# When side transfers and weight splits run in a linear attention and mixture-of-experts kernel: zeros and w2's copies in k's later quarters, w1 between wk and wv

## The chip, the cores and the metric

The kernel runs on one core of a Trainium2 chip. Its engines are TensorE (PE; PEld is its weight load), VectorE (DVE), ScalarE (ACT), GpSimd (POOL) and SyncE (SP, which only issues transfers). Each works through its own instruction queue in order. The metric is the device time of one execution, in microseconds; less is better.

## The reference

There are 2048 rows (tokens) of 512 values. A linear attention with 32 heads of 64 is followed by a mixture of 8 experts, of which each token uses 2. Everything is float32.

```python
x = hidden_states                                   # 2048 x 512
xn = layernorm(x)
q, k, v = relu(xn @ Wq), relu(xn @ Wk), xn @ Wv      # 2048 x 2048 each
kv = einsum('bhsd,bhse->bhde', k, v)
key_sum = k.sum(axis=2)
normalizer = clip(einsum('bhsd,bhd->bhs', q, key_sum), 1e-6)
x = x + (einsum('bhsd,bhde->bhse', q, kv) / normalizer) @ Wo + bo
xn = layernorm(x)
top_scores, top_idx = top_k(xn @ gate_w.T + gate_b + bias, 2)
gates = softmax(top_scores)
h = silu(einsum('td,ehd->teh', xn, w1) + b1)         # 8 experts, 352 hidden
x = x + sum over the two experts of gate * (h @ w2 + b2)
```

## The kernel before

Products keep float32's precision by splitting each operand into a high and a low half. The high half is a cast on ScalarE, the low half a subtraction on VectorE or GpSimd (`split`, both on L164), and each product is three matmuls (`mm3`, L158 to L160). There are 16 row tiles of 128 rows (`NT`), and k, v and q are worked on in four quarters of 512 columns (`NQ`).

The first part runs `a_step(s)` for s = 0 to 63; j = s // 16 is the quarter and t = s % 16 the row tile. In the first quarter a step also loads x two tiles ahead, normalises the next row tile (`a_norm`, which calls `norm`), transposes it into `xT` and writes its halves to memory (`xnd`); in later quarters the halves are read back a step ahead (`a_xn`, tile `xn_hl`). Each step then does:

- `a_k(s)`: twelve matmuls into `pk`; ScalarE's relu gives k's high half (L283), VectorE the low half (L284) and the running sum `kacc`.
- `a_g(s-1)`: twelve matmuls of the step before, k against xn, into the four banks `g`.
- At t = 2 of the next quarter, `a_kv(j-1)`: wv's slot against `g`, copied out as `kvs`, split and written to memory (`kvd`), and then the sums of k: `kacc` is split into `ka`, two matmuls with `ones` add over the rows into `pks`, and ScalarE copies the result to `ksb`.

Beside these the steps carry work for later. wk's next quarter is loaded at t = 8 and split at t = 9 to 12; wv is loaded at t = 12 and split at t = 13 and 14; in the first quarter GpSimd takes the low halves. The 22 chunks of w1 (512 columns each) are split in the consecutive steps 16 to 37: load a chunk to a `raw` buffer, split it into the one tile `stage`, write both halves to `w1d`. A chunk's load is held until the relu of the step before:

```python
hold([raw_load(("w1", w + 1), w1[:, ts(w + 1, 512)])], k_done[s - 1])
```

`hold` adds an order and no data; `k_done[s]` is the relu of step s.

After step 1 GpSimd gets its preparation, through `Late`, which holds each of its instructions until step 1's relu. In program order the zeros stand in it: 31 transfers of zeros into `out` behind the result rows, 15 into spare blocks of `xs_d` (with one column rewritten for each, in the same tile `zero`), and three copies of w2's experts with their b2 to `w2d`. Their transfers go through the software queue (q0), SP's through the hardware queue (q1).

This first part and the next, where q is worked on for 48 steps, are ordered on each engine by a planner that simulates the program; the program's order is the priority. The last sixteen steps of q and all the experts are ordered by hand. In q's part, `b_x1` loads x and GpSimd adds bo to it (L351); `b_n` uses `ksb`. `a_kv(3)` is called there at s = 1. The spare blocks, the zeros in `out` and `w2d` are read only by the experts.

Of the kernel before, what the change touches and what calls it, by code (L numbers as in the profile page):

```python
# [10 lines left out]
FP = mybir.dt.float32  # L11
# [4 lines left out]
AF = mybir.ActivationFunctionType  # L16
ALU = mybir.AluOpType
# [4 lines left out]
P = 128  # L22
# [4 lines left out]
def linear_attention__then__moe_kernel(  # L27
# [38 lines left out]
    nc = tc.nc  # L66
    S, C = x.shape
# [85 lines left out]
    def aux_bank(name):  # L153
        return ps.tile([P, 512], FP, tag="aux", bufs=2, name=name)
# [11 lines left out]
    def hold(held, behind):  # L166

        after = mybir.DependencyInfo(mybir.DependencyClass.Sync, mybir.DependencyReason.SCHED_ONLY)
        for ins in held:
            tc.add_manual_dep(ins.ins, behind.ins.name, after, reason="order")  # L170

    def words(engine, o, i):

        engine.dma_start(o.bitcast(FP), i.bitcast(FP))
# [30 lines left out]
    def raw_load(key, src):  # L205
        raws[key] = rawp.tile([P, CP], FP, tag="raw", bufs=4, name="raw")[:, 0:512]
        return nc.sync.dma_start(raws[key], src)

    def raw_split(key, hi, lo, on=nc.vector):
        return split(hi, lo, raws.pop(key), on)  # L210
# [4 lines left out]
    load_x(1)  # L215


    def norm(xt, dst):
        sm = const.tile([P, 16], FP, tag="sm", bufs=3, name="sm")
        st, mv, sd, rs = sm[:, 0:6], sm[:, 6:8], sm[:, 8:9], sm[:, 9:10]  # L220
        first = nc.vector.bn_stats(st, xt)
        nc.vector.bn_aggr(mv, st)
        root = nc.scalar.activation(sd, mv[:, 1:2], AF.Sqrt, bias=eps)
        nc.vector.reciprocal(rs, sd)
        last = nc.vector.tensor_scalar(dst, xt, mv[:, 0:1], rs, ALU.subtract, ALU.mult)
        return first, root, last

    def norm_sums(xt, more):
# [25 lines left out]

    def a_norm(t):
        xn = fpb.tile([P, C], FP, tag="xn", bufs=3, name="xn")
        ins = norm(xs.pop(t), xn)
        tp3 = transpose4(xn, "xtp")
        b, tt = divmod(t, TT)
        ins += split(xT[b][:, 0, :, ts(tt, P)], xT[b][:, 1, :, ts(tt, P)], tp3)  # L260
        xns[t] = frw.tile([P, 2, C], FR, tag="xs", bufs=3, name="xn_hl")
        ins += split(xns[t][:, 0, :], xns[t][:, 1, :], xn)
        words(nc.sync, xnd[t], xns[t])
        return ins
# [46 lines left out]
    def a_kv(j):  # L311

        for p0 in range(0, PP, 2):
            pkv = aux_bank("pkv").rearrange("p (a l b) -> p a l b", a=2, l=2)
            for p in range(p0, p0 + 2):
                for c in range(CC):
                    w, g = slot_n[0][:, c], slot_n[1][:, c]
                    nc.tensor.matmul(
                        pkv[:, p - p0], w[:, 0, ts(p, P)], g[:, :, ts(p, P)],
                        start=c == 0, stop=False,  # L320
                    )
                    nc.tensor.matmul(
                        pkv[:, p - p0, 0, :], w[:, 1, ts(p, P)], g[:, 0, ts(p, P)],
                        start=False, stop=c == CC - 1,
                    )
            for r in range(0, P, D):
                o = slice(r, r + D)
                kv = fpb.tile([P, 2, D], FP, tag="kvs", bufs=2, name="kvs")[o]
                nc.scalar.copy(kv, pkv[o, :, 1, o])
                nc.vector.tensor_add(kv, kv, pkv[o, :, 0, o])  # L330
                split(kvt[o, 0, p0 : p0 + 2, o], kvt[o, 1, p0 : p0 + 2, o], kv)
        words(nc.sync, kvd[j], kvt)
        pks = aux_bank("pks")
        ka = frw.tile([P, 2, QW], FR, tag="xs", bufs=3, name="ka")
        split(ka[:, 0, :], ka[:, 1, :], kacc[j])
        for l in range(2):
            nc.tensor.matmul(pks, ones, ka[:, l, :], start=l == 0, stop=l == 1)
        ksb[j] = fpb.tile([P, QW], FP, tag="ksb", bufs=NQ, name="ksb")
        nc.scalar.copy(ksb[j], pks)
# [196 lines left out]
    hold([n0[6]], n0[4])  # L536
    hold([wk0[2][0], wk0[3][0], n0[5]], n0[3])
    n_w1 = W1N // 512
    NC = 2
    k_done = {}  # L540

    def a_step(s):
        j, t = divmod(s, NT)
        if j == 0:
            if t + 2 < NT:
                load_x(t + 2)
            if t + 1 < NT:
                ins = a_norm(t + 1)
                hold([ins[0]], normed[t][2 if t else 4])
                normed[t + 1] = ins  # L550
        if s + 1 >= NT and s + 1 < NQ * NT:
            a_xn(s + 1)

        if t == 8 and j + 1 < NQ:
            for c in range(CC):
                hold([raw_load(("k", j + 1, c), wk[ts(c, P), ts(j + 1, QW)])], k_done[s - 1])
        if t in (9, 10, 11, 12) and j + 1 < NQ:
            c = t - 9
            w = slot_s[(j + 1) % 2]
            raw_split(  # L560
                ("k", j + 1, c), w[:, c, 0, :], w[:, c, 1, :], nc.vector if j else nc.gpsimd
            )
        if t == 9 and j == NQ - 1:
            for c in range(CC):
                raw_load(("q", 0, c), wq[ts(c, P), ts(0, QW)])
        if t in (10, 11, 12, 13) and j == NQ - 1:
            c = t - 10
            raw_split(("q", 0, c), slot_s[0][:, c, 0, :], slot_s[0][:, c, 1, :])
        if t == 12:
            for c in range(CC):  # L570
                raw_load(("v", j, c), wv[ts(c, P), ts(j, QW)])
        if t in (13, 14):
            for c in (2 * t - 26, 2 * t - 25):
                raw_split(
                    ("v", j, c), slot_n[0][:, c, 0, :], slot_n[0][:, c, 1, :],
                    nc.vector if j else nc.gpsimd,
                )

        w = s - NT
        if 0 <= w < n_w1:  # L580
            if w == 0:
                hold([raw_load(("w1", 0), w1[:, ts(0, 512)])], k_done[s - 1])
            raw_split(("w1", w), stage[:, 0, :], stage[:, 1, :])
            for l in range(2):
                words(nc.sync, w1d[l][:, ts(w, 512)], stage[:, l, :])
            if w + 1 < n_w1:
                hold([raw_load(("w1", w + 1), w1[:, ts(w + 1, 512)])], k_done[s - 1])
        k_done[s] = a_k(s)
        if s:
            a_g(s - 1)  # L590
        if j and t == 2:
            a_kv(j - 1)

    for s in range(NC):
        a_step(s)
# [20 lines left out]
    def temp():  # L616
        return fp1.tile([P, CX], FP, tag="f1", bufs=F1B, name="temp")
# [47 lines left out]
    m_all = rc.tile([P, NT, E], BF, name="m_all")  # L665
    nc.vector.memset(m_all, 0.0)
    place = const.tile([P, NT, 2], I32, name="place")

    zero = temp()
    pool.memset(zero[:, 0 : C + 1], 0.0)  # L670
    pool.memset(zero[:, C + 1 : C + 2], -1.0)
    for b in range(NT + NZ):
        pool.dma_start(out[S + b * P : S + (b + 1) * P, :], zero[:, 0:C])
    for b in range(NZ):
        pool.tensor_scalar(zero[:, C + 2 : CX], part, float(2 * S + b * P), None, ALU.add)
        pool.dma_start(xs_b[NB + b], zero)
    for e in range(E2):
        pool.dma_start(w2d[e, 0:HF].bitcast(FP), w2[e])
        pool.dma_start(w2d[e, HF : HF + 1].bitcast(FP), b2[e : e + 1, :])
    gb = temp()[:, 0 : 2 * E].rearrange("p (l e) -> p l e", l=2)  # L680
    pool.dma_start(gb[:, 0, :], gate_b.partition_broadcast(P))
    pool.dma_start(gb[:, 1, :], bias.partition_broadcast(P))
# [18 lines left out]
    pool.tensor_add(b1m, b1h, b1r)  # L701
    pool.memset(area[:, 80 * KB : 84 * KB].bitcast(FP), 0.0)

    for s in range(NC, NQ * NT):
        a_step(s)
    b_x1(0)
    b_x1(1)
    a_g(NQ * NT - 1)
# [154 lines left out]
    for s in range(NS - NT):  # L863
        j, t = divmod(s, NT)
        b_x1(s + 2)
        b_q(s)
        b_n(s)
        if s == 0:
            for p in range(PP):
                load_o(0, p)  # L870
            b_w(0, 0)
        if s == 1:
            a_kv(NQ - 1)
            for p in range(PP):
                if p + 1 < PP:
                    b_w(0, p + 1)
                b_m(0, p)
        if s >= 2:
            b_o(s - 2)
            for _ in b_add(s - 2):  # L880
                pass
        if s >= 1:
            b_t(s - 1)
        if t == 4:
            for c in range(CC):
                raw_load(("q", j + 1, c), wq[ts(c, P), ts(j + 1, QW)])
        if t in (5, 6, 7, 8):
            c = t - 5
            w = slot_s[(j + 1) % 2]
            raw_split(("q", j + 1, c), w[:, c, 0, :], w[:, c, 1, :])  # L890
        if t == 9:
            for p in range(PP):
                load_o(j + 1, p)
        if t in (10, 11, 12, 13):
            b_w(j + 1, t - 10)
            b_m(j + 1, t - 10)
# [346 lines left out]
```

## Time and profile before

| | us |
|---|---|
| median of 3 runs | 1022.81 |
| lowest and highest run | 1021.46, 1025.57 |
| profiled execution: its own time | 1025.18 |
| profiled execution: span from first to last instruction | 1023.4 |
| TensorE busy | 988.2 (97%) |
| VectorE busy | 559.7 (55%) |
| ScalarE busy | 345.1 (34%) |
| GpSimd busy | 190.8 (19%) |
| mean granted TensorE clock | 0.989 |

The durations of single instructions come from the one profiled execution, which ran 2.4 us above the median. A busy TensorE is not TensorE at its peak: matmuls overlap, and a row's duration (0.39 us for 512 columns) is longer than the distance from one start to the next (0.23 us). So steps are measured here from start to start of `pk`'s first matmul. In the timelines, a bracket at a row's end gives the idle time before it and what ended it.

### The profile page before, as it was taken

To read this page: it belongs to the slowest core of one execution; us is meant where nothing else is said; L and a number is where in the kernel's file an instruction comes from. 1 tells how busy PE (TensorE), PEld (TensorE's weight loads), DVE (VectorE), ACT (ScalarE), POOL (GpSimd) and SP (SyncE) were. 2 spreads that over 40 slices of the span, in tenths; PEclk is the share of its full clock that TensorE was granted. 3 is DMA by queue.
4 is the path that set the end of the run, shared out by engine and by line. 5 is a ranking of instruction groups with operands and counts; after the bars stand their busy time and mean duration, and the time that the engine had idled before them with its cause. 6 is when DMAs were issued, how large, how long until landed. Compare 5 with 4: busy or idle time off the path is not lost. (4 is left out here: it accounts for less than half of the span.)

```text
span 1023.4 us, 14704 instructions
## 1 busy us (share of the span) xinstructions
PE 988.2 (97%) x4903; PEld 825.8 (81%) x4903; DVE 559.7 (55%) x1382; ACT 345.1 (34%) x677; POOL 190.8 (19%) x225
## 2 busy tenths in 40 slices
PE   8999999999999999999999999999999989999993
PEld 5878877788888888788888888888888877889983
DVE  7873334453344226758656865766787766223330
ACT  4333222332223114324112411223545546444441
POOL 3653120000000010031000000001333210643354
PEclk9999999999999999999999999999999999999997
DMA  6994877865535242344322332348655697976788
GB/s 224 374 349 168 247 271 248 275 230 192 173 124 160 98 130 97 113 134 154 114 93 93 114 103 91 95 160 277 216 190 208 227 318 229 167 113 109 129 150 130
DMA packets 77898, 181.33 MB, mean 177 GB/s; under 512 B 9576, under 2 KB 12936, under 8 KB 77648
## 3 DMA queue, kind: packets, MB, share of 16 engines
q1 hardware_dynamic: 62240, 131.94, 39.2%
q0 software_dynamic: 15584, 48.44, 18.8%
q8 instruction: 43, 0.70, 0.3%
q14 instruction: 31, 0.25, 0.1%
HBM read 108.98 MB, written 79.83 MB: 184 GB/s over the span
## 5 line engine op out<-in xcount | busy, mean ns | idle before, releaser
L284 DVE SCALAR_TENSOR_TENSOR k<-pk,k 128x512 fp32r<-128x512 f32 x64 | 44.0, 687 | 122.1 <-ACT k L283 121.8
L158 PE MATMUL po<-area,qT 128*128 128x512 f32 x256 | 101.6, 397 | 1.5 <-ACT qT L164 1.5
L158 PE MATMUL pq<-area 128*128 128x512 f32 x256 | 102.6, 401 | 0.0
L158 PE MATMUL pk<-area 128*128 128x512 f32 x256 | 101.2, 395 | 0.8 <-ACT area L164 0.7
L160 PE MATMUL pk<-area 128*128 128x512 f32 x256 | 100.0, 391 | 1.0 <-DVE area L164 1.0
L159 PE MATMUL g<-k,xn_hl 128*128 128x512 f32 x256 | 100.8, 394 | 0.1
L160 PE MATMUL pq<-area 128*128 128x512 f32 x256 | 100.6, 393 | 0.0
L160 PE MATMUL g<-k,xn_hl 128*128 128x512 f32 x256 | 100.4, 392 | 0.0
L159 PE MATMUL pk<-area 128*128 128x512 f32 x256 | 99.9, 390 | 0.5 <-POOL area L164 0.3
L159 PE MATMUL pq<-area 128*128 128x512 f32 x256 | 100.3, 392 | 0.0
L159 PE MATMUL po<-area,qT 128*128 128x512 f32 x256 | 99.8, 390 | 0.0
L160 PE MATMUL po<-area,qT 128*128 128x512 f32 x256 | 98.7, 391 | 0.0
L164 ACT CAST qT<-qtp 128x512 fp32r<-128x512 f32 x64 | 36.7, 587 | 176.1 <-PE qtp L249 176.1
L158 PE MATMUL g<-k,xn_hl 128*128 128x512 f32 x256 | 91.0, 394 | 3.6 <-ACT k L283 3.6
L164 ACT CAST area<-raw 128x512 fp32r<-128x512 f32 x86 | 53.1, 621 | 117.4 <-DMA raw<-in_w 62.9
L164 DVE TENSOR_TENSOR area<-raw,area 128x512 fp32r<-128x512 f32 x77 | 53.6, 703 | 65.5 <-ACT area L164 54.7
L1132 POOL DMA_INDIRECT out<-ys,dest x37 | 58.2, 1573 | 119.6 <-ACT ys L1129 107.9
L351 POOL TENSOR_TENSOR x<-x,bo_b 128x512 f32<-128x512 f32 x16 | 21.4, 1348 | 311.9 <-DMA x<-in_x 306.7
L283 ACT ACTIVATE k<-pk 128x512 fp32r<-128x512 f32 x64 | 38.1, 596 | 121.9 <-PE pk L160 121.7
L369 DVE TENSOR_TENSOR qk<-q,ksb 128x512 f32<-128x512 f32 x64 | 44.4, 694 | 32.3 <-ACT q L361 31.6
L412 DVE TENSOR_TENSOR x<-x,po 128x512 f32<-128x512 f32 x48 | 32.9, 686 | 53.0 <-PE po L160 46.6
L361 ACT ACTIVATE q<-pq 128x512 f32<-128x512 f32 x64 | 38.4, 600 | 66.7 <-PE pq L160 42.5
(225 smaller groups left out, 2092.2 us busy)
## 6 DMA issues: line engine op xcount, KB each, us to landing
xn_hl<-xnd SPq DMA_DIRECT2D x48, 512.0 KB
x1d<-x SPq DMA_DIRECT2D x48, 256.0 KB
x<-x1d SPq DMA_DIRECT2D x48, 256.0 KB
w1d<-area SPq DMA_DIRECT2D x44, 256.0 KB
area<-w1d POOLq DMA_DIRECT2D x16, 704.0 KB
xg<-xs_d SPq DMA_DIRECT2D x37, 257.5 KB
xnd<-xn_hl SPq DMA_DIRECT2D x16, 512.0 KB
out<-temp POOLq DMA_DIRECT2D x31, 256.0 KB
```

The lines of the kernel that those rows point to most:

```text
L158: first = nc.tensor.matmul(o, lh, rh, start=start, stop=False)
L159: nc.tensor.matmul(o, lh, rl, start=False, stop=False)
L160: nc.tensor.matmul(o, ll, rh, start=False, stop=stop)
L164: return nc.scalar.copy(hi, src), on.tensor_sub(lo, src, hi.bitcast(FP))
L283: relu = nc.scalar.activation(k[:, 0, :], pk, AF.Relu)
L284: nc.vector.scalar_tensor_tensor(k[:, 1, :], pk, 0.0, k[:, 0, :].bitcast(FP), ALU.max, ALU.subtract)
L351: nc.gpsimd.tensor_add(x1s[s], x1s[s], bo_b)
L361: nc.scalar.activation(q, pq, AF.Relu)
L369: nc.vector.tensor_mul(qk, q, ksb[j])
L412: nc.vector.tensor_add(x1, x1, pos.pop(s))
L1132: added[i] = nc.gpsimd.indirect_dma_start(out[:, :], bass.IndirectOffsetOnAxis(dest[:, i : i + 1].bitcast(U32), 0), ys, None, compute_op=A ...
```

## The change

It moves work in time and between engines:

- The zeros and w2's copies leave the preparation. They become a list of 49 jobs (3 copies, 15 zero rows, 31 zero results), of which each step from 32 on takes two and holds them until its own relu.
- w1's 22 chunks are split in the steps from 16 on with t in 1, 3 to 8, or 15: 17, 19 to 24, 31, 33, 35 to 40, 47, 49, 51 to 55.
- In the first quarter wk is loaded at t = 5 and split at t = 6 to 9, and wv is loaded at t = 10 and split at t = 11 to 14, one chunk a step. VectorE takes all their low halves.
- The sums of k become `a_ks`, called at t = 6 instead of in `a_kv` at t = 2; for the last quarter at s = 6 of q's part instead of s = 1.
- `norm` gets a flag. For row tiles 6 to 15 the last step (x - mean) * rs is a ScalarE activation with scale rs and bias -mean * rs, and VectorE computes that bias.

```diff
-    def norm(xt, dst):
+    def norm(xt, dst, on_scalar):
...
-        last = nc.vector.tensor_scalar(dst, xt, mv[:, 0:1], rs, ALU.subtract, ALU.mult)
+        if on_scalar:
+            nc.vector.scalar_tensor_tensor(nr, mv[:, 0:1], -1.0, rs, ALU.mult, ALU.mult)
+            last = nc.scalar.activation(dst, xt, AF.Identity, bias=nr, scale=rs)
+        else:
+            last = nc.vector.tensor_scalar(dst, xt, mv[:, 0:1], rs, ALU.subtract, ALU.mult)
...
-        ins = norm(xs.pop(t), xn)
+        ins = norm(xs.pop(t), xn, t > 5)
...
         words(nc.sync, kvd[j], kvt)
+
+    def a_ks(j):
+
         pks = aux_bank("pks")
...
+    w1_steps = [
+        s for s in range(NT, NQ * NT) if s % NT in (1, 3, 4, 5, 6, 7, 8, NT - 1)
+    ][:n_w1]
...
-        if t == 8 and j + 1 < NQ:
+        t_k, t_v = (9, 12) if j else (6, 10)
+        if t == t_k - 1 and j + 1 < NQ:
...
-        if t in (9, 10, 11, 12) and j + 1 < NQ:
-            c = t - 9
+        if t_k <= t < t_k + CC and j + 1 < NQ:
+            c = t - t_k
             w = slot_s[(j + 1) % 2]
-            raw_split(
-                ("k", j + 1, c), w[:, c, 0, :], w[:, c, 1, :], nc.vector if j else nc.gpsimd
-            )
+            raw_split(("k", j + 1, c), w[:, c, 0, :], w[:, c, 1, :])
...
-        if t == 12:
+        if t == t_v:
...
-        if t in (13, 14):
-            for c in (2 * t - 26, 2 * t - 25):
...
+        if t > t_v:
+            parts_v = (t - t_v - 1,) if not j else (2 * (t - t_v) - 2, 2 * (t - t_v) - 1)
...
-        w = s - NT
-        if 0 <= w < n_w1:
-            if w == 0:
-                hold([raw_load(("w1", 0), w1[:, ts(0, 512)])], k_done[s - 1])
+        if s in w1_steps:
+            w = w1_steps.index(s)
             raw_split(("w1", w), stage[:, 0, :], stage[:, 1, :])
...
-            if w + 1 < n_w1:
-                hold([raw_load(("w1", w + 1), w1[:, ts(w + 1, 512)])], k_done[s - 1])
+        if s + 1 in w1_steps:
+            w = w1_steps.index(s + 1)
+            hold([raw_load(("w1", w), w1[:, ts(w, 512)])], k_done[s - 1])
...
+        if j and t == 6:
+            a_ks(j - 1)
...
-    for b in range(NT + NZ):
-        pool.dma_start(out[S + b * P : S + (b + 1) * P, :], zero[:, 0:C])
-    for b in range(NZ):
-        pool.tensor_scalar(zero[:, C + 2 : CX], part, float(2 * S + b * P), None, ALU.add)
-        pool.dma_start(xs_b[NB + b], zero)
-    for e in range(E2):
-        pool.dma_start(w2d[e, 0:HF].bitcast(FP), w2[e])
...
+    later = [
+        *((copy_weights, e) for e in range(E2)), *((zero_rows, b) for b in range(NZ)),
+        *((zero_results, b) for b in range(NT + NZ)),
+    ]
+
     for s in range(NC, NQ * NT):
         a_step(s)
+        if s >= 2 * NT:
+            for job, n in later[:2]:
+                hold(job(n), k_done[s])
+            del later[:2]
...
+        if s == 6:
+            a_ks(NQ - 1)
```

More of the change, by code (lines that the diff above doesn't have):

```diff
@@ L215, in linear_attention__then__moe_kernel @@
     load_x(1)
-    def norm(xt, dst):
+    def norm(xt, dst, on_scalar):
         sm = const.tile([P, 16], FP, tag="sm", bufs=3, name="sm")
-        st, mv, sd, rs = sm[:, 0:6], sm[:, 6:8], sm[:, 8:9], sm[:, 9:10]
+        st, mv, sd, rs, nr = sm[:, 0:6], sm[:, 6:8], sm[:, 8:9], sm[:, 9:10], sm[:, 10:11]
         first = nc.vector.bn_stats(st, xt)
@@ L568, in a_step @@
             raw_split(("q", 0, c), slot_s[0][:, c, 0, :], slot_s[0][:, c, 1, :])
-        if t == 12:
+        if t == t_v:
             for c in range(CC):
                 raw_load(("v", j, c), wv[ts(c, P), ts(j, QW)])
-        if t in (13, 14):
-            for c in (2 * t - 26, 2 * t - 25):
[L574 to L577, printed above, removed]
-        w = s - NT
-        if 0 <= w < n_w1:
-            if w == 0:
-                hold([raw_load(("w1", 0), w1[:, ts(0, 512)])], k_done[s - 1])
+        if t > t_v:
+            parts_v = (t - t_v - 1,) if not j else (2 * (t - t_v) - 2, 2 * (t - t_v) - 1)
+            for c in parts_v:
+                if c < CC:
+                    raw_split(("v", j, c), slot_n[0][:, c, 0, :], slot_n[0][:, c, 1, :])
+        if s in w1_steps:
+            w = w1_steps.index(s)
             raw_split(("w1", w), stage[:, 0, :], stage[:, 1, :])
@@ L667, in linear_attention__then__moe_kernel @@
     place = const.tile([P, NT, 2], I32, name="place")
-    zero = temp()
-    pool.memset(zero[:, 0 : C + 1], 0.0)
-    pool.memset(zero[:, C + 1 : C + 2], -1.0)
-    for b in range(NT + NZ):
-        pool.dma_start(out[S + b * P : S + (b + 1) * P, :], zero[:, 0:C])
-    for b in range(NZ):
-        pool.tensor_scalar(zero[:, C + 2 : CX], part, float(2 * S + b * P), None, ALU.add)
-        pool.dma_start(xs_b[NB + b], zero)
-    for e in range(E2):
-        pool.dma_start(w2d[e, 0:HF].bitcast(FP), w2[e])
-        pool.dma_start(w2d[e, HF : HF + 1].bitcast(FP), b2[e : e + 1, :])
     gb = temp()[:, 0 : 2 * E].rearrange("p (l e) -> p l e", l=2)
@@ L702, in linear_attention__then__moe_kernel, with zero_results, zero_rows, copy_weights @@
     pool.memset(area[:, 80 * KB : 84 * KB].bitcast(FP), 0.0)
+    zero = temp()
+    pool.memset(zero[:, 0 : C + 1], 0.0)
+    pool.memset(zero[:, C + 1 : C + 2], -1.0)
+    def zero_results(b):
+        return [nc.gpsimd.dma_start(out[S + b * P : S + (b + 1) * P, :], zero[:, 0:C])]
+    def zero_rows(b):
+        to = float(2 * S + b * P)
+        return [
+            nc.gpsimd.tensor_scalar(zero[:, C + 2 : CX], part, to, None, ALU.add),
+            nc.gpsimd.dma_start(xs_b[NB + b], zero),
+        ]
+    def copy_weights(e):
+        return [
+            nc.gpsimd.dma_start(w2d[e, 0:HF].bitcast(FP), w2[e]),
+            nc.gpsimd.dma_start(w2d[e, HF : HF + 1].bitcast(FP), b2[e : e + 1, :]),
+        ]
+    later = [
+        *((copy_weights, e) for e in range(E2)), *((zero_rows, b) for b in range(NZ)),
+        *((zero_results, b) for b in range(NT + NZ)),
+    ]
     for s in range(NC, NQ * NT):
         a_step(s)
+        if s >= 2 * NT:
+            for job, n in later[:2]:
+                hold(job(n), k_done[s])
+            del later[:2]
+    assert not later
     b_x1(0)
```

## The prediction

> **What bounds the kernel now.** I read the busy shares of the page first, then the table of stretches, then TensorE's waits, and last the timelines of TensorE and ScalarE around its longest waits.
>
> ```profile
> PE 988.2 (97%) x4903; PEld 825.8 (81%) x4903; DVE 559.7 (55%) x1382; ACT 345.1 (34%) x677; POOL 190.8 (19%) x225
> ...
> PE   8999999999999999999999999999999989999993
> ```
>
> TensorE is busy for 97% of the span, so an edit pays only where TensorE waits or runs slowly. The second row (40 slices) shows where: at the ends, and in the table below.
>
> ```profile
> 30.00:62.00 32.00, 32.00 (x153) 26.48 (x152) 24.19 (x56) 10.23 (x22) 17.82 (x34) 1.00 1.02 392
> 100.00:150.00 50.00, 48.23 (x228) 40.10 (x227) 19.01 (x35) 14.27 (x30) 7.40 (x18) 1.00 0.80 260
> 150.00:200.00 50.00, 47.25 (x196) 37.06 (x195) 21.64 (x34) 14.05 (x25) 4.83 (x5) 0.97 0.80 259
> 200.00:235.00 35.00, 35.00 (x171) 29.59 (x170) 17.49 (x32) 12.30 (x26) 0.00 (x0) 1.00 0.71 246
> 165.00:168.50 3.50, 3.50 (x10) 2.74 (x9) 0.69 (x1) 0.59 (x1) 0.00 (x0) 0.52 0.56 167
> ```
>
> Columns: stretch, its length, busy PE, PEld, DVE, ACT, POOL (with instructions), granted clock, DMA share, GB/s. From 30 to 62 us, while the zeros stream out, DMA is full, yet TensorE is gapless. It idles in k's second quarter (100 to 200 us), and the last row shows a stretch at half clock.
>
> ```profile
> PE g L158 <- ACT k L283: 3.6, 4, 1.8
> ...
> PE pks L337 <- DVE kvs L330: 1.8, 1, 1.8
> ```
>
> Total us, times, longest. TensorE waits for the relu of k, and once for the bank of the sums of k. Why the relu is late stands on ScalarE's timeline:
>
> ```profile
> 149.03 0.62 ACT L164 CAST area<-raw 128x512 fp32r<-128x512 f32 x1 [4.56 <-DMA raw<-in_w]
> 149.55 0.59 ACT L283 ACTIVATE k<-pk 128x512 fp32r<-128x512 f32 x1
> 154.38 0.62 ACT L164 CAST area<-raw 128x512 fp32r<-128x512 f32 x1 [4.24 <-DMA raw<-in_w]
> 154.91 0.60 ACT L283 ACTIVATE k<-pk 128x512 fp32r<-128x512 f32 x1
> 160.39 2.60 ACT L164 CAST area<-raw 128x512 fp32r<-128x512 f32 x4 [4.88 <-DMA raw<-in_wk]
> 162.89 0.59 ACT L283 ACTIVATE k<-pk 128x512 fp32r<-128x512 f32 x1
> ```
>
> Every relu is queued behind the cast of a chunk of w1, and that cast waits for the chunk's load, which is held until the relu before. This is a loop: relu, load, cast, relu. At 160 us wk's casts stand in it too. TensorE then shows the price:
>
> ```profile
> 161.36 0.39 PE L160 MATMUL pk<-area 128*128 128x512 f32 x1
> 163.54 0.73 PE L158 MATMUL g<-k,xn_hl 128*128 128x512 f32 x2 [1.79 <-ACT k L283]
> ...
> 165.64 0.63 PE L158 MATMUL g<-k,xn_hl 128*128 128x512 f32 x1
> ```
>
> After the 1.79 us wait come matmuls of 0.63 us instead of 0.39: the half clock.
>
> **What is there to win.** I take the starts of pk's first matmul of successive steps. An undisturbed step has 24 matmuls and lasts 5.44 us (136.88 to 142.32). Over that, the second quarter loses 9.33 - 5.44 = 3.89 (158.87 to 168.20, the wait and the half clock), 6.86 - 5.44 = 1.42 (184.97 to 191.83, where wv's casts stand in the loop), and 0.23 + 0.21 + 0.24 = 0.68 in three others. The step with the sums of k lasts 8.03 (123.41 to 131.44), against 6.01 in the next quarter (222.68 to 228.69): 2.02. In the first quarter, where a step with its four transposes lasts 5.92, one lasts 7.23 (67.41 to 74.64) while wk's four casts (62.75 to 68.85) stand ahead of a relu: 1.31. Sum 3.89 + 1.42 + 0.68 + 2.02 + 1.31 = 9.32 us. This is nearly all that the change can win. One wait of 1.24 us for qT at 418 us, beside the last a_kv, may go as well, since the last sums of k leave that place: 0 to 1.3, and I take 0.
>
> **w1 in steps without wk or wv; zeros gone from the second quarter.** With zeros the loop's period, from the relu starts 137.08, 143.87, 149.55, 154.91, is 6.79, 5.68 and 5.36, mean 5.94, over the 5.44 of a step. Without zeros, after 192 us (192.65, 197.78, 202.58, 207.23, 212.06), it is 5.13, 4.80, 4.65, 4.83. So in steps 19 to 24 ScalarE would catch up instead of falling behind, and wk and wv find it on time. A relu may start about 4.5 us after its matmuls' end before TensorE notices (it has the next step's pk and the g before to do, 5.44, less relu and k's low half). With wk the loop took 162.89 - 154.91 = 7.98, that is 2.5 late: within the 4.5. I count 3.89, 1.42 and 0.68 as won.
>
> **wk and wv of the first quarter.** The loads go out at steps 5 and 10, and the casts are spread over steps 6 to 9 and 11 to 14. Eight low halves move from GpSimd (1.29 each) to VectorE (0.70 each, 5.6 us). VectorE is busy 24.19 of 32 and 19.90 of 38 us there, and ten rows of the norm leave it: 10 x (0.64 - 0.14) = 5 us. Cost 0 under that cover; without it, the 1.0 that pk waited once for a low half. On SP's queue wk's four loads now stand ahead of x's next load, held until step 4's relu; x is loaded two steps ahead, so 0, at most one step's slip of the norm's 0.6. The 1.31 is won, because wk comes one chunk to a step and without zeros in the way.
>
> **Norms on ScalarE.** Ten of them at 0.82 (the row of the same operation at L243), about 8 us, beside 10.23 + 15.05 busy in the 70 us from 30 to 100. The row's chain grows by 0.14 + (0.82 - 0.64) = 0.3 us, but a row is normalised a step ahead of its use. I take 0; if each of the ten were on the path, 3.
>
> **Sums of k at t = 6.** The two matmuls stay (6.01 - 5.44 = 0.57). At t = 2 the wait on the banks of kv goes: 2.02 won. New is that the cast of ka now stands on ScalarE among the casts of w1 (t = 3 to 8) in three quarters, and pks has no step of slack, unlike g: TensorE, in order, holds the next pk behind it. Bounds: 0, and 2.0 each (the old wait), so 0 to 6. I take 1.5: nothing in the second quarter, where the loop is shorter than a step, and 0.75 in each of the others.
>
> **Zeros and copies in quarters three and four.** GpSimd shows 0.00 busy from 200 to 235 us, so its queue is free; its next work, adding bo, comes at 369.68, and two jobs a step from step 32 are through by step 56, at about 350. The 15 zero rows wait for one another as before (each rewrites the tile that the last one sends; starts 119.67, 123.70, 128.47), so steps 35 to 40 get the loop of 5.94: (5.94 - 5.44) x 6 = 3.0 late, then wk's 2.5, together 5.5, of which 1.0 is over the slack of 4.5. I take 1.0, bounds 0 and the old 3.89. In steps 51 to 55 two zero results of 0.262 MB run beside w1: at the 420 GB/s of the fullest slices between 30 and 62 us they delay a load by at most 1.25; the period is then 4.85 + 1.25 = 6.1, and 5 x 0.66 = 3.3 stays under 4.5. I take 0; with 6.79 in each, 5 x 1.35 - 4.5 = 2.3. The three copies of w2 (0.72 MB each, 1.7 us at that rate) meet one chunk of w1: 0, at most 3.4.
>
> **Sum.** -9.32 + 1.5 + 1.0 = -6.8 us. The profiled execution took 1025.18 us, its span 1023.4; the changed one should take 1018.4, span 1016.6. The median of the runs is 1022.81, 2.4 below the profiled one, which is where I apply it: 1016.0.
>
> [...]
>
> **Rivals.**
>
> *The stalls move with the zeros* (0.24; no difference). In k's third quarter the same zero rows meet the same kind of steps, w1 and then wk: the 3.89 comes back there, and pks waits 2.0 in two quarters instead of 0.75. Gain 9.32 - 3.89 - 4.0 = 1.4, about 1021.4. For it: the loop with zero rows is over 5.44. Against it: six chunks in a row instead of sixteen.
>
> *The two DMA queues share the engines* (0.13; slower). Between 30 and 62 us the software queue (zeros) took 58.9% of the engines and left the hardware queue 5.35 MB in 32 us, 167 GB/s. A step with w1 moves 1.31 MB there (xn_hl 512 KB, a chunk of 256 KB and two writes), which would take 7.85 us instead of 5.44. All the moved bytes, 31 x 0.262 + 15 x 0.264 + 3 x 0.72 = 14.2 MB at the 223 GB/s that the software queue had, last 64 us, or 8.1 such steps: 8.1 x 2.4 = 19.5 lost, less 9.3 won, about 1033. It decides once the zeros hold their share for more than half of those 64 us. Against it: from 100 to 150 us zero rows and w1 ran together at 0.80 DMA share with steps of 5.44.
>
> [...]
>
> **How the numbers follow.** The forecast has 0.63, from 1012 (nothing new, and the qT wait gone: -10.6) to 1017.7. A difference under about 0.5%, 5.1 us, cannot be told from none here. So: faster 0.63, same 0.24, slower 0.13. The range is 1012 to 1024: above the forecast it takes in the first rival, and the second as far as the point where the zeros cost what the rest wins; it leaves out the rest of the second and cases better than every term.
>
> **What would show it.** Right: no wait of g for k's relu between 100 and 200 us, no half clock near 165, steps of 5.44 there and 6.01 for the one with pks; GpSimd empty from about 60 to 195 us and busy to 350. Wrong: waits of pks for ka at t = 6 over 0.75 us (then that term), g waiting after step 40 (third quarter), steps over 5.44 in 51 to 55 with DMA at 0.9 (queues), or xtp waiting for xn between 45 and 95 us (norms).

## The result, and the profile after

The changed kernel takes 1019.18 us (median of 22 runs, 1014.88 to 1023.81), the kernel before 1022.31 (22 runs, 1020.63 to 1026.76): a ratio of 0.9967, 95% interval 0.9954 to 0.998, so 2 to 5 us less. The forecast was 6.8 less. The measured 3.1 is also under the 5.1 us below which the forecast counted a difference as none, an outcome that it gave 0.24; its first choice, faster by more than that, did not come. The profiled execution of the changed kernel took 1018.25 us with a span of 1016.5, which is where the forecast put it; but that is luck, the gap between an execution of before that lay 2.9 us above its median and one of after that lay 0.9 below.

The stretches of the changed kernel, in the columns of before:

```profile
30.00:62.00 32.00, 32.00 (x154) 26.50 (x153) 24.09 (x55) 19.09 (x37) 5.63 (x8) 1.00 0.58 197
100.00:150.00 50.00, 50.00 (x238) 41.99 (x237) 20.77 (x37) 14.16 (x29) 0.00 (x0) 1.00 0.61 209
150.00:200.00 50.00, 50.00 (x223) 41.39 (x222) 20.61 (x32) 13.80 (x24) 2.11 (x4) 1.00 0.56 191
200.00:235.00 35.00, 35.00 (x171) 29.58 (x170) 11.17 (x23) 8.08 (x19) 6.21 (x14) 1.00 0.83 265
240.00:260.00 20.00, 18.22 (x73) 14.57 (x72) 10.75 (x17) 7.15 (x13) 2.84 (x8) 0.91 0.82 277
325.00:345.00 20.00, 18.50 (x82) 15.01 (x81) 11.06 (x18) 7.97 (x14) 3.67 (x7) 1.00 0.97 334
```

The second quarter (100 to 200 us) is gapless, with the DMA share down from 0.80 to about 0.6. New are two stretches in which TensorE idles 1.8 and 1.5 us, one with a lowered clock (0.91), both with the engines' share at 0.82 to 0.97. TensorE's waits up to 400 us (line, waited for; total us, times, longest):

```profile
PE g L158 <- ACT k L287: 4.2, 4, 1.8
PE pw L531 <- DVE idle L528: 1.3, 1, 1.3
PE pk L158 <- ACT area L164: 0.7, 1, 0.7
```

The wait of pks is gone, the waits of g for k's relu are not. They have moved. TensorE, then ScalarE around the first of them:

```profile
247.94 0.39 PE L160 MATMUL pk<-area 128*128 128x512 f32 x1
250.10 1.19 PE L158 MATMUL g<-k,xn_hl 128*128 128x512 f32 x4 [1.78 <-ACT k L287]
...
251.59 0.62 PE L159 MATMUL g<-k,xn_hl 128*128 128x512 f32 x1
```

```profile
234.75 0.59 ACT L287 ACTIVATE k<-pk 128x512 fp32r<-128x512 f32 x1
...
239.30 0.62 ACT L164 CAST area<-raw 128x512 fp32r<-128x512 f32 x1 [3.44 <-DMA raw<-in_w]
239.82 0.59 ACT L287 ACTIVATE k<-pk 128x512 fp32r<-128x512 f32 x1
245.72 0.62 ACT L164 CAST area<-raw 128x512 fp32r<-128x512 f32 x1 [5.31 <-DMA raw<-in_wk]
...
248.94 0.62 ACT L164 CAST area<-raw 128x512 fp32r<-128x512 f32 x1 [1.06 <-DMA raw<-in_wk]
249.46 0.59 ACT L287 ACTIVATE k<-pk 128x512 fp32r<-128x512 f32 x1
```

It is the picture that before had at 160 us, one quarter later: the relu of step 40 stands behind casts that wait for wk, 9.64 us after the relu of step 39, and the half clock follows (0.62 us a matmul; granted clock 0.50 from 251.59 to 255.00 us). At 331 us it is wq's casts, behind a chunk of w1:

```profile
329.81 0.62 ACT L164 CAST area<-raw 128x512 fp32r<-128x512 f32 x1 [5.18 <-DMA raw<-in_w]
...
332.27 0.62 ACT L164 CAST area<-raw 128x512 fp32r<-128x512 f32 x1 [0.55 <-DMA raw<-in_wq]
```

For all kernels I read four points off ScalarE's timeline, the starts of the relus of steps 16, 32, 48 and 63, and give the time between them. A relu may itself be late without a wait of TensorE, so single quarters can shift by some us; the sum from 16 to 63 is what counts, and 268.3 is the value without any wait.

| kernel | start of 16 | 16 to 32 | 32 to 48 | 48 to 63 | 16 to 63 |
|---|---|---|---|---|---|
| before, two profiles | 106.3, 104.8 | 100.9, 99.3 | 89.7, 90.5 | 85.8, 85.8 | 276.4, 275.6 |
| after, two profiles | 103.9, 103.6 | 91.3, 91.3 | 95.4, 96.3 | 87.2, 90.0 | 273.8, 277.6 |
| only_zeros | 104.1 | 97.3 | 90.8 | 85.8 | 274.0 |
| only_w1 | 105.2 | 94.0 | 91.3 | 85.8 | 271.1 |
| jobs_in_q | 104.5 | 91.3 | 91.3 | 85.8 | 268.3 |
| q_w1_16_37 | 103.7 | 95.6 | 89.0 | 85.8 | 270.5 |
| q_first | 106.2 | 91.3 | 91.3 | 85.8 | 268.4 |
| q_norm_vector | 105.6 | 91.3 | 91.3 | 85.8 | 268.3 |
| q_sums_at_2 | 103.6 | 91.3 | 91.3 | 85.8 | 268.3 |
| results_in_q | 104.7 | 91.3 | 95.7 | 85.8 | 272.8 |
| jobs_between | 104.3 | 91.3 | 93.5 | 88.1 | 272.8 |
| w1_not_at_8 | 104.1 | 91.3 | 96.2 | 86.6 | 274.1 |

### The profile page after: what moved, and what is told of

It is laid out like the page before. It is cut to its first block, busy times and chain, and to the rows that moved or that the text cites. A ratio compares the mean times of both kernels' runs of the same rounds, so it can differ in the third digit from the quotient of the medians.

```text
span 1016.5 us, 14704 instructions
## 1 busy us (share of the span) xinstructions
PE 986.2 (97%) x4903; PEld 825.4 (81%) x4903; DVE 555.1 (55%) x1390; ACT 352.1 (35%) x687; POOL 180.5 (18%) x217
## 4 chain that ended last, share of the span: by engine, by line
PE 81%; DMA 9%; DVE 4%; ACT 3%; issue 1%; SPq 1%; POOL 0%; POOLq 0%; ACTq 0%; DVEq 0%
PE pq L158 6%; PE pq L160 6%; PE pq L159 6%; PE po L158 6%; PE po L160 5%; PE po L159 5%; PE g L158 5%; PE g L160 5%; PE g L159 5%; PE pk L158 4%; PE pk L159 4%; PE pk L160 4%; DMA raw<-in_w 4%; PE qtp L253 3%; PE py L158 2%; PE py L159 2%
## 5 line engine op out<-in xcount | busy, mean ns | idle before, releaser
L164 DVE TENSOR_TENSOR area<-raw,area 128x512 fp32r<-128x512 f32 x85 | 57.7, 688 | 107.6 <-ACT area L164 107.4
L158 PEld LDWEIGHTS g<-k,xn_hl 128*128 128x128 f32 x256 | 47.5, 188 | 15.3 <-ACT k L287 5.8
L158 PEld LDWEIGHTS pk<-area 128*128 128x128 f32 x256 | 48.2, 188 | 10.6 <-ACT area L164 0.9
L160 PEld LDWEIGHTS pk<-area 128*128 128x128 f32 x256 | 48.2, 188 | 10.5 <-DVE area L164 0.4
```

The lines of the kernel that those rows point to most:

```text
L158: first = nc.tensor.matmul(o, lh, rh, start=start, stop=False)
L160: nc.tensor.matmul(o, ll, rh, start=False, stop=stop)
L164: return nc.scalar.copy(hi, src), on.tensor_sub(lo, src, hi.bitcast(FP))
```

## The experiments

The theory: relu, load, cast, relu is a loop, and zeros beside w1 lengthen it past a step (in before 5.94 us with zeros and 4.85 without, a step 5.44). The rival that most of these runs test against it is not one of the prediction's: the loads of wk, wv and wq meet w1 in that loop, and that costs with or without zeros.

**after_again and before_again**, both kernels unaltered.

> The changed kernel once more, unaltered, to see which of its waits are its own and which are chance. If the waits of g for the relu of k near 248 us (1.9) and 331 us (1.7) belong to the order of the work, both are here again within 0.5 us. If chance made them, at least one is gone. Half clock: one stretch of 3.4 us before 800 us if it follows the wait at 248, otherwise at another place or none.

Measured: 0.999 of before (0.9973 to 1.0008), so these twelve runs alone show no gain. Both waits are there, but larger than the 0.5 us allowed; here the first is put down to another thing. TensorE's waits, SyncE's issue of the halves of xn, TensorE's wait for them, and ScalarE's relu of step 40:

```profile
PE g L158 <- DMA xn_hl<-xnd: 3.4, 1, 3.4
PE g L158 <- ACT k L287: 3.2, 3, 2.2
```

```profile
243.49 1.47 SPq L174 DMA_DIRECT2D xn_hl<-xnd  x2
```

```profile
251.37 1.62 PE L158 MATMUL g<-k,xn_hl 128*128 128x512 f32 x3 [3.37 <-DMA xn_hl<-xnd]
```

```profile
250.54 0.59 ACT L287 ACTIVATE k<-pk 128x512 fp32r<-128x512 f32 x1
```

The halves of xn were issued behind four loads of wk, by 244.96 us, and g started at 251.37: 6.4 us for 2 x 512 KB, with zero rows beside them. But the relu of step 40 ended only at 251.13, 0.2 us before g started. A punctual xn_hl would have won no more than that: this wait too is in the main the late relu's. Half clock followed both waits (granted clock 0.91 from 240 to 260 us and from 325 to 345). From step 16 to 63 one profile of the changed kernel lost 5.5 us, the other 9.3: the waits belong to the order, their size to chance.

> The kernel before once more, unaltered. If its waits belong to the order of the work, g waits near 161 and 187 us, pks near 128 and pk near 67 us again, each within 0.7 us, and the second quarter from relu to relu is 100 to 101 us. If chance makes them, the second quarter differs by over 2 us.

Measured: the same places, with 1.2 us for pks, 1.6 for g near 160 us and 0.7 for pk near 67. The second quarter is 99.3, below the 100 to 101 expected; the wait near 187 us was 0.25 instead of 0.9. The profile that the forecast was built on thus showed a little more loss than this one: from 16 to 63 it lost 8.1 us, this one 7.3.

**jobs_in_q**: the 49 jobs leave k's quarters.

```diff
-        if s >= 2 * NT:
-            for job, n in later[:2]:
-                hold(job(n), k_done[s])
-            del later[:2]
...
         b_q(s)
+        if s >= 8:
+            for job, n in later[:2]:
+                hold(job(n), q_done[s])
+            del later[:2]
```

> The zeros and the copies of w2 go two to a step behind q's relu, from step 8 of q's part on, instead of into k's quarters. Loop theory (zeros beside w1 lengthen relu, load, cast, relu over a step's 5.44): both waits of g (1.9 and 1.7) and the half clock behind the first vanish, 5 us less than the changed kernel, and none comes in q's part, where no relu stands behind a load that it releases. Rival (the first loads of wk and wq stand in the loop with w1, zeros or not): both waits stay within 0.5 us and the time is that of the changed kernel.

Measured: 1012.75 us beside 1022.21 for the changed kernel and 1023.88 for before, measured together; the ratio to before is 0.9893 (0.9876 to 0.991). Its waits up to 400 us, and its stretches, the last one in q's part with the jobs:

```profile
PE pw L533 <- DVE idle L530: 1.3, 1, 1.3
PE g L158 <- ACT k L287: 1.0, 2, 0.7
PE pk L158 <- ACT area L164: 0.7, 1, 0.7
```

```profile
240.00:260.00 20.00, 20.00 (x90) 16.58 (x89) 9.14 (x14) 7.24 (x13) 0.00 (x0) 1.00 0.67 228
325.00:345.00 20.00, 20.00 (x90) 16.55 (x89) 10.98 (x17) 7.95 (x14) 0.00 (x0) 1.00 0.76 262
430.00:530.00 100.00, 100.00 (x474) 83.00 (x473) 67.69 (x125) 25.73 (x46) 36.46 (x59) 1.00 0.64 210
```

Only the waits of the first 20 us are left, and the clock is full (1.00 in the stretches shown). The theory had 5 us, from the first profile of the changed kernel, which lost 5.5 from 16 to 63; the runs gave 9.5, near the 9.3 of the second. The 100 us of q's part shown take the jobs without a gap: no chunk of w1 is in their way. This version beats both kernels.

**only_zeros** and **only_w1**: before with one part each.

```diff
-    for b in range(NT + NZ):
-        pool.dma_start(out[S + b * P : S + (b + 1) * P, :], zero[:, 0:C])
...
+    later = [
...
     for s in range(NC, NQ * NT):
         a_step(s)
+        if s >= 2 * NT:
+            for job, n in later[:2]:
+                hold(job(n), k_done[s])
+            del later[:2]
```

> The kernel before with one part of the change: zeros and copies two to a step from step 32 on; w1, wk, wv, the sums and the norms as before. Loop theory: in k's second quarter the loop is 4.65 to 5.13, so the waits near 161 (1.8) and 187 us (0.9) and most of that of the sums (1.8) vanish, 6 us of the 9.3 are won, and steps 32 to 37, which have w1 and zeros, show under 1 us. Rival (w1 meets wk and wv in the same steps, zeros or not): the waits near 161 and 187 stay within 0.5 us, and no more than 2 us are won.

Measured: 0.9954 (0.9937 to 0.9971), 5 us less. From 16 to 63 only 1.6 to 2.4 us of it are won, not the 6 that the theory had.

```profile
PE g L158 <- ACT k L283: 2.8, 4, 1.0
...
PE pks L337 <- DVE kvs L330: 1.1, 1, 1.1
```

The wait near 161 us went, as the theory had it, but two of 1.0 and 0.9 us stand at 174 and 181 us, where wv's casts meet w1: there the rival was right. pks waited 1.1 in the third quarter instead, at 222 us, where w1 still ran beside zero rows.

```diff
+    w1_steps = [
+        s for s in range(NT, NQ * NT) if s % NT in (1, 3, 4, 5, 6, 7, 8, NT - 1)
+    ][:n_w1]
...
-        w = s - NT
-        if 0 <= w < n_w1:
...
+        if s in w1_steps:
+            w = w1_steps.index(s)
...
```

> The kernel before with one part of the change: w1 in the steps with t of 1, 3 to 8 and 15; zeros, wk, wv, sums and norms as before. Loop theory: zeros still lengthen the loop in steps 17 to 24 (5.94), so about 1 us of wait stays where wk comes (near 161), that of wv (187) vanishes, and 3 to 4 us are won. Rival (w1 meets wk and wv): the waits near 161 and 187 both vanish, as w1 is out of the way of all but wk's loads, 5 to 6 us are won.

Measured: 0.995 (0.993 to 0.997), 5 us less. One wait of 1.5 us is left where wk comes, at 158 us, and none at wv and pks. The place and size of the wait are the theory's; the gain (16 to 63: 271.1, better than the whole change) is 4.5 to 5.3 us there, above its 3 to 4.

**q_w1_16_37, q_first, q_norm_vector, q_sums_at_2**: jobs_in_q with one other part undone each (the edit of the first, without that of jobs_in_q).

```diff
-    w1_steps = [
-        s for s in range(NT, NQ * NT) if s % NT in (1, 3, 4, 5, 6, 7, 8, NT - 1)
-    ][:n_w1]
+    w1_steps = list(range(NT, NT + n_w1))
```

> The jobs stay in q's part, and w1 goes back to the consecutive steps 16 to 37 (still never at the steps of the zeros). If zeros alone lengthened the loop, the second quarter stays at 91.3 us from the relu of step 16 to that of step 32 and the time is that with the jobs in q's part, 1012.8. If w1 standing with wk and wv costs by itself, waits of g of 1 to 1.5 us come near wk (155 to 160) and wv (175 to 185), the second quarter is 94 to 97 us, and the time is 3 to 6 us more.

Measured: 0.9916 (0.9902 to 0.993); 270.5 from 16 to 63, so 2.2 lost, with one wait of 1.1 us near 180 us at wv. The spread of w1 earns about 2 us by itself; with the zeros in the second quarter it earned more.

> The jobs stay in q's part, and in the first quarter wk and wv go back to steps 8 to 12 and 12 to 14 with GpSimd's low halves. If the 1.3 us that the kernel before lost near 67 us came from zeros in the way of wk's loads, nothing is lost (1012.8). If it came from four casts in a row ahead of the relu, whatever the transfers, 1 to 1.5 us come back there.

Measured: 0.9923 (0.9899 to 0.9947). The named wait of pk near 68 us is only 0.3, but the steps that start at 61.53 and 67.66 us last 6.13 and 6.82 instead of 5.93: 1.1 us lost without any zeros, as the second theory had it. (Step 16 starts 1.7 later than in jobs_in_q; the other 0.6 had been lost before 16 us.) In only_zeros, where the norms stay on VectorE, the old order loses 0.3 there, so the size is 0.3 to 1.1.

> The jobs stay in q's part, and all norms end on VectorE as in the kernel before. By the forecast ScalarE's part is worth nothing: the same within 1 us (1012.8), no wait of xtp for xn. Rival: VectorE, which now has the low halves of wk and wv too, falls behind in steps 6 to 15, TensorE waits for a low half of xT or k, and 1 to 3 us are lost there.

Measured: 0.9899 (0.9879 to 0.9919), and 268.3: the norms on ScalarE are worth nothing that these runs show.

> The jobs stay in q's part, and the sums of k go back to t = 2, right behind kv. With no chunk of w1 split at t = 2 and no zeros, ScalarE is on time there: if the old 2.0 us came from ScalarE standing at w1's load, pks waits under 0.5 us and the time is the same (1012.8). If the two banks of kv are the cause by themselves, pks waits 1 to 2 us in the three quarters, 3 to 6 us in all.

Measured: 0.9887 (0.9871 to 0.9903), no wait of pks. With no chunk of w1 at t = 2, the sums can stay there. only_w1, which has no chunk there either but keeps the zeros, has no such wait; only_zeros has one in the third quarter, where zeros run beside w1, and none in the second. So the wait came from ScalarE standing at the load of a chunk that other transfers delay.

**results_in_q, jobs_between, w1_not_at_8**: which neighbour makes the new waits.

```diff
-        if s >= 2 * NT:
+        if 2 * NT <= s < 2 * NT + 9:
...
```

The 31 zero results follow in q's part, as in jobs_in_q.

> The changed kernel with the 31 zero results moved to q's part; the 3 copies and 15 zero rows stay two to a step from step 32 on. If each wait belongs to the transfers next to it, the one near 331 us (results) vanishes and the one near 248 us (rows, where wk comes) stays at 1.5 to 3.5 us: third quarter 95 to 96 us from relu to relu, fourth 85.8. If both come from a lateness that rows and copies alone start, both stay; if from results alone, both vanish.

Measured: 0.992 (0.9892 to 0.9948), third quarter 95.7, fourth 85.8. The wait near 331 us is gone, the one near 248 stays:

```profile
251.94 1.22 PE L158 MATMUL g<-k,xn_hl 128*128 128x512 f32 x2 [2.60 <-ACT k L287]
```

So the wait at 331 us belongs to the zero results beside it, and the one at 248 needs only the copies and zero rows.

```diff
-        if s >= 2 * NT:
-            for job, n in later[:2]:
+        if s >= 2 * NT and s % NT in (0, 9, 10, 11, 12, 13, 14, 15):
+            for job, n in later[:4]:
...
+            del later[:4]
```

> The changed kernel with its 49 jobs kept in k's third and fourth quarters, but four to a step and only in the steps without a chunk of w1 (t of 0 and 9 to 15). If the cost is zeros beside w1's loads in the loop, the waits near 248 and 331 us vanish and the time is that with the jobs in q's part, 10 us under the kernel before. If the cost is the engines' share as such (xn_hl late), g waits for xn_hl in some step of t 9 to 15, 2 to 4 us each, and the gain is 3 to 7.

Measured: 0.9966 (0.9948 to 0.9984). The wait near 248 us is gone, one of 2.4 us stands at 331. The plan did not hold: GpSimd's queue shows why.

```profile
298.76 0.59 POOL L714 DMA_DIRECT2D xs_d<-temp  x1 [0.31 <-POOL temp L713]
304.09 0.21 POOL L713 TENSOR_SCALAR temp<-part 128x1 f32<-128x1 f32 x1 [4.73 <-DMA xs_d<-temp]
...
318.44 0.59 POOL L714 DMA_DIRECT2D xs_d<-temp  x1 [0.30 <-POOL temp L713]
```

Each zero row waits for the one before it to leave the tile (4.73 us), so four a step fall behind, and rows ran until 318 us beside w1's chunks of the fourth quarter. ScalarE then reached wq late. So only the third quarter, where no row was sent from 200 to 253 us, is the clean separation that was planned.

```diff
-        s for s in range(NT, NQ * NT) if s % NT in (1, 3, 4, 5, 6, 7, 8, NT - 1)
+        s for s in range(NT, NQ * NT) if s % NT in (0, 1, 3, 4, 5, 6, 7, NT - 1)
```

> The changed kernel with the chunk of w1 at t = 8 moved to t = 0, so that no chunk is split in the step in which wk is loaded; zeros stay in k's third and fourth quarters. Rival (wk's first load meets w1 in the loop): the wait near 248 us vanishes, the one near 331 (wq) stays. Loop theory: one chunk fewer ahead of wk is 0.5 us less lateness, so 1 to 3 us of wait near 248 stays; the time is within 2 us of the changed kernel.

Measured: 0.9977 (0.9965 to 0.999). Near 248 us there is no wait, as the rival had it. But pk waits 1.6 for `kacc` at 293 us, where the chunk at t = 0 now waits 7.93 us for its load beside zero results, and g waits 1.7 near 327. So the wait at 248 needs both: the jobs (jobs_in_q has none with the chunk at t = 8) and that chunk (this run has none with the jobs). Taking the chunk away moved the loss to the next chunk that stood beside zeros.

## Why the prediction was right in direction, and where its size was off

**What is there to win: right.** The 9.3 us were found: jobs_in_q, which has every other part of the change, is 0.9893 of before, 9 to 13 us, and the second quarter falls to 91.3 us in every kernel with both the zeros away and w1 spread. Neither part alone does it (97.3 and 94.0), as the loop has it: zeros make it long, wk and wv meet it. In the changed kernel the signs named for the second quarter came: no wait of g between 100 and 200 us and no half clock near 165 (granted clock 1.00 from 155 to 172 us).

**First quarter, 1.31:** the wait near 67 us is gone. How it divides between the zeros and the four casts in a row is open: only_zeros loses 0.3 there, q_first 1.1. **Norms at 0:** right. **The qT wait, taken as 0:** it fell from 1.24 to 0.2 in the changed kernel, so about 1 us more was won; it came back (1.2) in q_sums_at_2, so it is the last sums' place beside a_kv that makes it.

**Sums of k, taken as 1.5: measured 0.** No profile of after shows pks waiting.

**Zeros and copies in quarters three and four, taken as 1.0: measured 5.5 and 9.3.** This is the step that failed. The sign that the prediction named for it came: g waits after step 40.

The first term missed is the copies of w2, taken as 0. The chunk of w1 of step 33 was loaded while the third copy went out, with the first zero row behind it, and ScalarE waited 7.23 us for it. In jobs_in_q, which has no copies there, it waited 2.82. GpSimd's issue and ScalarE in the changed kernel, then ScalarE in jobs_in_q:

```profile
201.51 0.49 POOL L719 DMA_DIRECT2D w2d<-in_w  x1 [3.33 <-ACT k L287]
```

```profile
208.46 0.62 ACT L164 CAST area<-raw 128x512 fp32r<-128x512 f32 x1 [7.23 <-DMA raw<-in_w]
208.98 0.59 ACT L287 ACTIVATE k<-pk 128x512 fp32r<-128x512 f32 x1
```

```profile
204.62 0.62 ACT L164 CAST area<-raw 128x512 fp32r<-128x512 f32 x1 [2.82 <-DMA raw<-in_w]
```

The relu of step 34 then started 2.95 us after the end of its matmuls, instead of 0.04 in jobs_in_q. The relus of steps 35 to 39 kept this lateness (2.8 to 3.6 us). The forecast had 3.0 us late by step 40 as well, but from the zero rows of steps 35 to 40; there the loop took 5.39 a step (218.26 to 239.82, relu of 35 to that of 39), a step's length, and added nothing. That the two agree is luck. No run keeps the zero rows and leaves out the copies, so how much of the 2.95 us is the copies' and how much the first row's stays open.

The second is the loop with wk. I took it as 7.98 from before, where the last zero row had left by 150.12 us, ahead of wk's loads; here it was 9.64 beside zero rows, and 8.60 in jobs_in_q without any. The relu of step 40 was then 6.58 us late, more than the slack (4.8 us, by the 1.78 that g waited; the forecast took 4.5). In w1_not_at_8 the relu of step 39 was on time, wk's loop took 9.46, and there was no wait: the lateness from step 33 and wk are needed together.

The third is the half clock, by my estimate 1.7 each (3.41 us at a granted clock of 0.50): it stood in the loss of before but not in that of after, and fell once in one profile (0.91 from 240 to 260 us, 1.00 from 325 to 345) and twice in the other (0.91 in both). The fourth is wq: its loads are not held, the planner put them at step 54, so its casts stood in w1's loop (324.03 to 332.80, 8.77), which my sum for the fourth quarter, 0, did not contain.

From 16 to 63 the two profiles of before lost 8.1 and 7.3, those of after 5.5 and 9.3: about 0.3 won on the mean. With some 1.8 by the start of step 16 and 1 at qT that is 3.1, the measured difference; but the same profiles differ by another 1 us after step 63, so the split is rough and its agreement in part luck. The prediction's first rival (the stalls move with the zeros, 1021.4) was nearer to the measured median than the forecast. Its second (the two queues share the engines, 1033) did not come: beside zero rows TensorE was gapless from 200 to 235 us at a DMA share of 0.83.

## What to carry to other kernels

A load that ScalarE waits for ahead of a relu that TensorE needs is a loop: the relu of step 40 stood behind such casts and started 6.58 us after its matmuls. Keep its mean period under a step (here 5.44 us) and count the transfers beside it: ScalarE waited 7.23 us for a chunk beside w2's third copy and the first zero row, 2.82 without them. Moving transfers paid only where no such loop stood: the same bytes cost 5 to 9 us beside w1 and nothing in q's part. And losses read from one profile should be checked in a second one before they are set against a median.

## What the runs showed of the hardware

The granted clock was 0.50 from 165.13 to 168.54 us in before and from 251.59 to 255.00 us in after, 3.41 us each, and 1.00 in the 3.4 us ahead of and behind both. In the 3.4 us ahead TensorE was busy for 1.53 us in before and for 1.63 in after, so it had idled 1.89 and 1.78. Longer stretches, with the longest wait of TensorE in each:

| kernel | stretch, us | longest wait, us | granted clock |
|---|---|---|---|
| after_again | 240 to 260 | 3.37 (g) | 0.91 |
| after_again | 325 to 345 | 2.2 (g) | 0.91 |
| results_in_q | 245 to 260 | 2.60 (g) | 0.89 |
| jobs_between | 325 to 340 | 2.4 (g) | 0.89 |
| before_again | 155 to 170 | 1.6 (g) | 0.89 |
| before | 120 to 135 | 1.8 (pks) | 1.00 |
| w1_not_at_8 | 288 to 345 | 1.7 (g) | 1.00 |
| after | 330 to 340 | 1.50 (g) | 1.00 |

The length of one wait does not tell these stretches apart: 1.6 us stands among those with a lowered clock, 1.8 among those without. What else decides was not shown.
